# The gate of the experts' rows: both factors multiplied onto the MLP's result in PSUM, in place of one product in SBUF

## The chip, the cores and the metric

The kernel runs on one core of one Trainium2 chip, all in float32. A core has TensorE (PE; PEld is its weight load), VectorE (DVE), ScalarE (ACT), GpSimd (POOL) and a queue that issues DMAs (SP). Each engine runs its own instructions in program order and waits on the others by semaphores. The metric is the device time of one execution in microseconds (us): 1550.95 us before the change, the median of three runs (1548.26 to 1552.72).

## The reference, cut to what matters

```python
xn = layernorm(x)                                  # 2 x 2048 tokens of 256
s = mamba_and_mlp(xn)                              # x1 = xn + mamba(rmsnorm(xn)); s = x1 + mlp(rmsnorm(x1))
g = silu(moe(xn))                                  # 8 experts, the top 2 of each token, weighted
return x + s * g
```

`silu(v)` is `v * sigmoid(v)`, which is `h * (tanh(h) + 1)` with `h = v / 2`. The kernel holds `h` (the experts' two rows of a token, with weights that are already halved, added) in the tile `yk[0]` and `tanh(h)` in the tile `yk[1]`. The gate `g` thus has two factors, `yk[0]` and `yk[1] + 1`, and the last lines of the kernel compute `out = x + s * g`.

## The kernel before, in words

**Stages.** 4096 tokens are cut into 8 blocks (`c`) of 512. After an opening (norms, routing, the scatter of rows to experts) one long loop runs the Mamba recurrence: for each block, each of 4 groups of 128 channels (`d`) and each of 8 pairs of states (`g`), 256 steps in all. In each step DVE makes `b` (L1361, a product of `du` in PSUM and `B` in SBUF) and runs two scans into `h` (L1365); POOL multiplies `h` by `C` (L1295) and adds the pair (L1297); PE sums over the states into `y` in PSUM (L1267); ACT makes the exponentials `da` (L1254) and saves last columns (`hs`, L1291). At the start of each group DVE makes `du` from two SBUF tiles (L1358).

**Work drawn in beside it.** A generator hands out PE work of the feed-forward parts between the steps: first 39 tiles of 256 rows for the experts (`Expert`), then 16 tiles of 256 tokens for the MLP (`Mlp`, `c` and `hf`). The change touches only the last ones; in the trace their first multiplication starts at 1072.3 us, after the last of the experts. I number them 1 to 16.

**One MLP tile.** `pair` makes the hidden layer (PE `phm` L854, ACT tanh L1026, DVE product into `hidm` L1028); `second` multiplies with the second weights into `pom` (PE L866), in the PSUM bank "o", of which there is one, shared with the output projection of the Mamba part (`po`, L762). `gather` (L1044 on) has POOL issue four indirect DMAs of the experts' rows into `yk` (L1058), and puts later work on a list: `weigh` (ACT L1072, POOL addition L1076), `tanh` (ACT L1080) and `gate` (DVE L1083), due 5, 7 and 8 half-steps after the gather. There is a single pair of `yk` tiles: the next gather is issued only after `end` has cleared `yk_taken`, and its DMAs wait until the tile that they write was read for the last time.

**The end of one tile.** `finish` puts `total` (DVE L1094: `pom` times 0.5 plus `x1`), and that puts `end`: DVE L1101 (`pom` times `yk[0]`, which holds the whole gate by then), DVE L1102 (plus `x`, into an SBUF tile) and the store (SP L1105). If the gate has not been issued by then, `end` draws work from the list until it has.

**What sets the order.** `later` (class `Later`) is a list sorted by due time; `tick` and each half-step of the loop run what is due. The place of an instruction in its engine's queue is thus fixed when the program is built. In 11 of the 16 tiles the gate (L1083) stands directly ahead of L1101 in DVE's queue: `end` drew it there, or it was due there; in the tiles 3, 4, 6, 9 and 10 it stands earlier, with other DVE work between the two.

Of the kernel before, what the change touches and what calls it, by code (L numbers as in the profile page):

```python
# [11 lines left out]
ALU = mybir.AluOpType  # L12
# [37 lines left out]
def kernel(  # L50
# [18 lines left out]
    nc = tc.nc  # L69
# [107 lines left out]
    def act_table(name):  # L177

        if table[0] != name:
            nc.scalar.preload_act_table_set(name)  # L180
            table[0] = name
# [171 lines left out]
    later = Later()  # L353
# [12 lines left out]
    def drop(tag, n):  # L366
        gone.setdefault(tag, set()).add(n)
# [5 lines left out]
    def ring(tag, bufs):  # L373

        n = take(tag)
        later.free(tag, n - bufs)
        return tag, n
# [537 lines left out]
    class Expert(Ffn):  # L915
# [44 lines left out]
        def finish(self, po, n):  # L960
            i = self.i
            no = ring("ys", 2)
            expert_rows.append(no)
            ys = rows.tile([P, JS, DM], F32, tag="ys", name=f"ys{i}")
            later.put(
                lambda: nc.vector.tensor_tensor(  # L966
                    ys, po, self.b2.unsqueeze(1).to_broadcast([P, JS, DM]), ALU.add
                ),
                n, after=2,
            )  # L970
            later.put(
                lambda: nc.sync.dma_start(
                    ys_d[ts(i, TS), :].rearrange("(j p) d -> p j d", p=P), ys
                ),
                no, after=4,
            )
# [4 lines left out]
    class Mlp(Ffn):  # L981
# [61 lines left out]
        def gather(self):  # L1043

            c, hf = self.c, self.hf
            i0 = c * J + hf * JS
            yk_taken.append(self.name)
            if not yk_tiles:
                for k in range(TOPK):
                    yk_tiles.append(  # L1050
                        wpool.tile([P, JS, DM], F32, tag=f"w{k + 1}", name=f"yk{k}", bufs=5)
                    )
            yk = self.yk = yk_tiles
            for no in expert_rows:
                later.free(*no)
            for j in range(JS):
                for k in range(TOPK):
                    nc.gpsimd.indirect_dma_start(  # L1058
                        out=yk[k][:, j, :], out_offset=None, in_=ys_d,
                        in_offset=bass.IndirectOffsetOnAxis(  # L1060
                            ap=row_y[:, k, i0 + j : i0 + j + 1], axis=0
                        ),
                    )
            self.nxo = ring("ys", 2)
            self.xo = rows.tile([P, JS, DM], F32, tag="ys", name=f"xo{self.name}")
            self.tok = slice(c * T + hf * TS, c * T + (hf + 1) * TS)
            nc.sync.dma_start(self.xo, x[self.tok, :].rearrange("(j p) d -> p j d", p=P))

            def weigh():
                for j in range(JS):  # L1070
                    for k in range(TOPK):
                        nc.scalar.activation(  # L1072
                            yk[k][:, j, :], yk[k][:, j, :], AF.Copy,
                            scale=prob[:, k, i0 + j : i0 + j + 1],
                        )
                nc.gpsimd.tensor_tensor(yk[0], yk[0], yk[1], ALU.add)  # L1076

            def tanh():
                act_table(WITH_TANH)
                nc.scalar.activation(yk[1], yk[0], AF.Tanh)  # L1080

            def gate():
                nc.vector.scalar_tensor_tensor(yk[0], yk[1], 1.0, yk[0], ALU.add, ALU.mult)  # L1083
                self.gated = True

            later.put(weigh, after=5)
            later.put(tanh, after=7)
            later.put(gate, after=8)

        def finish(self, po, n):  # L1090
            x1, yk, xo = self.x1, self.yk, self.xo

            def total():
                nc.vector.scalar_tensor_tensor(po, po, 0.5, x1, ALU.mult, ALU.add)  # L1094
                drop("x1", self.n_x1)
                later.put(end, n)

            def end():
                while not self.gated:
                    later.next()  # L1100
                nc.vector.tensor_tensor(po, po, yk[0], ALU.mult)  # L1101
                nc.vector.tensor_tensor(xo, po, xo, ALU.add)  # L1102
                yk_taken.clear()
                later.put(
                    lambda: nc.sync.dma_start(  # L1105
                        out[self.tok, :].rearrange("(j p) d -> p j d", p=P), xo
                    ),
                    self.nxo, after=3,
                )

            later.put(total)
# [338 lines left out]
```

## Time and profile before

| | |
|---|---|
| median of three runs | 1550.95 us (1548.26 to 1552.72) |
| the profiled execution | 1551.53 us, its span 1549.8 us |
| mean granted TensorE clock | 0.948 |
| busy: PE, DVE, POOL, ACT | 1396.0, 1244.3, 1154.8, 919.8 us |
| DVE L1083, the gate, 16 times | 20.2 us, mean 1261 ns, from 665 to 2175 |
| idle of DVE just before L1083 | 13.8 us in 6 of them, on ACT's tanh |
| DVE L1101 and L1102, 16 times each | 11.1 us each |
| stage of the MLP tiles | from 1072.3 us; the last scan ends at 1486.3 us |

The span runs from the first to the last instruction of the profiled execution. "Idle before" is time in which the engine stood still ahead of an instruction, with what ended the wait. "Busy" contains whatever an instruction spends blocked once it has started, so that one and the same operation can show different durations.

### The profile page before, as it was taken

The numbers are of one execution on the slowest core, as the hardware profiler recorded it, in microseconds if no ns is written. First come the engines' busy times: TensorE is split into PE (matmuls) and PEld (weight loads), VectorE is DVE, ScalarE is ACT, GpSimd is POOL, SyncE is SP. The second block draws the span as 40 slices with busy tenths as digits, with TensorE's granted clock in tenths as the row PEclk, the third lists the DMA queues.
The fourth block names the chain that finished last, engine by engine and source line by source line (L and its number), as shares of the span: only waits on it lengthen the run. The fifth ranks groups of instructions, "written<-read, shape, count | busy, mean of one in ns | idle before, by whom it ended". The sixth has DMA issues, their size and how long they took to land. (4 is left out here: it accounts for less than half of the span.)

```text
span 1549.8 us, 18158 instructions
## 1 busy us (share of the span) xinstructions
PE 1396.0 (90%) x5246; PEld 982.9 (63%) x5246; DVE 1244.3 (80%) x1362; ACT 919.8 (59%) x1890; POOL 1154.8 (75%) x775
## 2 busy tenths in 40 slices
PE   6747999998999999999999999999888988899667
PEld 4524677666676577667766777667555656667436
DVE  7558887797788977799879777986898788899942
ACT  4846676575656764477557655676465664475322
POOL 2777689768786689679977897688865778677741
PEclk9558999999999999999999999999998999999888
DMA  5594347723592438524853467345610125412100
GB/s 188 206 378 162 94 141 250 268 86 110 165 343 86 129 115 288 199 87 144 271 214 118 129 217 283 92 125 186 225 48 27 49 68 208 131 35 68 55 14 28
DMA packets 171108, 233.70 MB, mean 151 GB/s; under 512 B 19824, under 2 KB 141552, under 8 KB 171008
## 3 DMA queue, kind: packets, MB, share of 16 engines
q1 hardware_dynamic: 164864, 215.75, 42.0%
q0 software_dynamic: 6144, 16.79, 3.2%
q8 instruction: 42, 0.69, 0.2%
q14 instruction: 58, 0.48, 0.1%
HBM read 196.04 MB, written 36.44 MB: 150 GB/s over the span
## 5 line engine op out<-in xcount | busy, mean ns | idle before, releaser
L1295 POOL TENSOR_TENSOR h<-h,C 128x1024 f32<-128x1024 f32 x256 | 608.7, 2379 | 230.9 <-ACT hs L1291 187.4
L1365 DVE TENSOR_TENSOR_SCAN h<-da,hs,b 128x512 f32<-128x512 f32 x384 | 479.0, 1271 | 42.7 <-PE y L1267 17.6
L1254 ACT ACTIVATE da<-dt,a_neg 128x512 f32<-128x512 f32 x512 | 358.2, 718 | 41.6 <-DVE h L1365 41.2
L1267 PE MATMUL y<-h,ident 128*128 128x512 f32 x594 | 304.9, 616 | 32.4 <-POOL h L1295 18.3
L1361 DVE TENSOR_TENSOR b<-du,B 128x1024 f32<-128x1024 f32 x256 | 314.7, 1229 | 19.3 <-DMA B<-bcd 13.3
L854 PE MATMUL phe<-xsTe,w_e 128*128 128x256 f32 x1248 | 290.8, 385 | 13.5 <-ACT hide L954 8.9
L854 PEld LDWEIGHTS phe<-xsTe,w_e 128*128 128x128 f32 x1248 | 239.1, 192 | 81.5 <-issue 25.6
L866 PE MATMUL poe<-w_e,hide 128*128 128x256 f32 x1248 | 289.2, 380 | 0.0
L1297 POOL TENSOR_TENSOR h<-h 128x512 f32<-128x512 f32 x215 | 276.4, 1286 | 16.9
L866 PEld LDWEIGHTS poe<-w_e,hide 128*128 128x128 f32 x1248 | 236.0, 191 | 65.1 <-issue 33.6
L954 ACT ACTIVATE hide<-phe,b 128x256 f32<-128x256 f32 x312 | 129.3, 469 | 129.3 <-PE phe L854 129.1
L1267 PEld LDWEIGHTS y<-h,ident 128*128 128x128 f32 x594 | 112.9, 197 | 122.9 <-issue 66.0
L1365 DVE TENSOR_TENSOR_SCAN h<-da,b 128x512 f32<-128x512 f32 x128 | 151.2, 1210 | 11.2 <-PE y L1267 3.2
L854 PE MATMUL phm<-xsTm,w_m 128*128 128x256 f32 x512 | 125.2, 397 | 21.4 <-DVE hidm L1028 20.8
L854 PEld LDWEIGHTS phm<-xsTm,w_m 128*128 128x128 f32 x512 | 100.6, 198 | 48.9 <-DVE hidm L1028 25.9
L866 PE MATMUL pom<-w_m,hidm 128*128 128x256 f32 x512 | 122.0, 390 | 3.1 <-DVE xom L1102 3.0
L866 PEld LDWEIGHTS pom<-w_m,hidm 128*128 128x128 f32 x512 | 100.0, 197 | 31.8 <-issue 14.4
L1291 ACT COPY hs<-h 128x2 f32<-128x2 f32 x192 | 36.1, 188 | 99.6 <-DVE h L1365 99.4
L459 POOL DMA_INDIRECT xs_d<-xt,slot x64 | 63.3, 989 | 38.7 <-DVE scratch L441 19.8
L1058 POOL DMA_INDIRECT yk<-ys_d,row_y x64 | 61.6, 962 | 38.6 <-DVE pom L1101 21.3
L582 DVE SCALAR_TENSOR_TENSOR xc<-px,par_sb,xc 128x512 f32<-128x512 f32 x96 | 71.5, 746 | 16.6 <-ACT xc L574 11.7
L966 DVE TENSOR_TENSOR ys<-poe,b 128x512 f32<-128x512 f32 x39 | 26.6, 682 | 58.8 <-PE poe L866 51.9
(175 smaller groups left out, 1438.3 us busy)
## 6 DMA issues: line engine op xcount, KB each, us to landing
w_e<-in_w SPq DMA_DIRECT2D x312, 256.0 KB, 3.5
B<-bcd SPq DMA_DIRECT2D x64, 512.0 KB, 6.9
C<-bcd SPq DMA_DIRECT2D x64, 512.0 KB, 7.3
xs<-xs_d SPq DMA_DIRECT2D x39, 256.0 KB, 2.7
ys_d<-ys SPq DMA_DIRECT2D x39, 256.0 KB, 4.2
b<-in_b SPq DMA_DIRECT2D x39, 128.0 KB, 4.1
xnr<-xnd SPq DMA_DIRECT2D x16, 256.0 KB, 7.5
xom<-in_x SPq DMA_DIRECT2D x16, 256.0 KB, 3.3
```

The lines of the kernel that those rows point to most:

```text
L459: r = nc.gpsimd.indirect_dma_start(out=xs_d, out_offset=bass.IndirectOffsetOnAxis(ap=slot[:, k, i : i + 1], axis=0), in_=x_of(i // J, i % ...
L582: nc.vector.scalar_tensor_tensor(v[:, s : s + T], px, conv_w[:, d, KC - 1 - s : KC - s], v[:, s : s + T], ALU.mult, ALU.add,)
L854: nc.tensor.matmul(ph[:, q, :], self.w1[c0 // 2][:, k, ts(q, P)], self.xT[:, k, :], start=(k == 0), stop=(k == KM - 1),)
L866: nc.tensor.matmul(po[:, j, :], self.hid[c // 2][:, c % 2, ts(j, P)], self.w2[c // 2][:, c % 2, :], start=(c == 0 and j == 0), stop=(c == ...
L954: nc.scalar.activation(hc[:, q, :], ph[:, q, :], AF.Relu, bias=self.b1[:, c0 + q : c0 + q + 1])
L1058: nc.gpsimd.indirect_dma_start(out=yk[k][:, j, :], out_offset=None, in_=ys_d, in_offset=bass.IndirectOffsetOnAxis(ap=row_y[:, k, i0 + j : ...
L1254: nc.scalar.activation(das[n][:, q, :], dts[c, d], AF.Exp, scale=a_neg[:, d, 2 * g + q : 2 * g + q + 1])
L1267: nc.tensor.matmul(ys[c, d], ident, hts[n][:, q, :], start=False, stop=(g == DS // 2 - 1 and q == nq - 1),)
L1295: nc.gpsimd.tensor_tensor(hts[n], hts[n], bct[c, "C", g], ALU.mult)
L1297: nc.gpsimd.tensor_tensor(hts[n][:, 0, :], hts[n][:, 0, :], hts[n][:, 1, :], ALU.add)
L1361: nc.vector.tensor_tensor(inp, dus[c, d].unsqueeze(1).to_broadcast([P, 2, T]), bct[c, "B", g], ALU.mult,)
L1365: nc.vector.tensor_tensor_scan(hts[n][:, q, :], das[n][:, q, :], inp[:, q, :], 0.0 if c % CPB == 0 else hs[c - 1][:, d, 2 * g + q : 2 * g ...
```

## The change

The product in SBUF is taken away, and its first factor goes onto `pom` in PSUM in `end`, as a third operation there. The tile counts as gated when the tanh is issued.

```diff
             def tanh():
                 act_table(WITH_TANH)
                 nc.scalar.activation(yk[1], yk[0], AF.Tanh)
-
-            def gate():
-                nc.vector.scalar_tensor_tensor(yk[0], yk[1], 1.0, yk[0], ALU.add, ALU.mult)
                 self.gated = True
 
             later.put(weigh, after=5)
             later.put(tanh, after=7)
-            later.put(gate, after=8)
...
             def end():
                 while not self.gated:
                     later.next()
+
+                nc.vector.scalar_tensor_tensor(po, yk[1], 1.0, po, ALU.add, ALU.mult)
                 nc.vector.tensor_tensor(po, po, yk[0], ALU.mult)
                 nc.vector.tensor_tensor(xo, po, xo, ALU.add)
```

The number of DVE instructions stays the same: 16 `scalar_tensor_tensor` from SBUF, SBUF to SBUF go, 16 from SBUF, PSUM to PSUM come. The queues of PE, ACT, POOL and SP keep all their instructions in the same order. DVE's queue differs only in the place of these 16: in 11 tiles the new one stands exactly where the old one stood, and in the tiles 3, 4, 6, 9 and 10 it moves later, to just ahead of L1101. The new operation waits for the tanh and for L1094; `yk[1]` is now read last by it, and `yk[0]` by L1101 as before.

## The prediction, blind

> **What bounds the kernel now.** I read the page first, then the source view of the gate's line, then the timeline around each of its 16 executions, and last what PE waited for. Times in parentheses are starts in the trace. No engine bounds alone: PE is busy for 90% of the span, DVE 80%, POOL 75%, and the chain that ended last passes from one to the other. The gate's line is on it:
>
> ```profile
> PE 18%; DVE 10%; POOL 8%; issue 4%; ACT 3%; DMA 1%; SPq 0%; DVEq 0%; POOLq 0%; ACTq 0%
> DVE h L1365 4%; PE y L1267 4%; POOL h L1295 3%; PE poe L866 3%; PE pom L866 3%; PE phe L854 2%; DVE b L1361 2%; PE phm L854 2%; PE po L762 2%; POOL yk L1058 2%; POOL h L1297 1%; DVE xc L582 1%; DVE yk L1083 1%; POOL ls L648 1%; POOL dt L649 1%
> ```
>
> One per cent of 1550 us is 16 us, and all of L1083 is 20.2 us busy. The next view is that of its line (least, middle and longest time in ns, then the idle time ahead of it):
>
> ```profile
> L1083 DVE SCALAR_TENSOR_TENSOR yk<-yk,yk x16: 665/892/2175, 1098.6 to 1544.6; 128x512 f32<-128x512 f32 x16
> ...
>   ACT yk L1080: 13.8, 6
> ```
>
> The same operation on tiles of one size takes 665 or 2175 ns. The timeline of tile 1 shows why (start, us, engine, line):
>
> ```profile
> 1097.85 2.36 POOL L1295 TENSOR_TENSOR h<-h,C 128x1024 f32<-128x1024 f32 x1
> ...
> 1098.59 2.16 DVE L1083 SCALAR_TENSOR_TENSOR yk<-yk,yk 128x512 f32<-128x512 f32 x1 [1.12 <-ACT yk L1080]
> ...
> 1100.79 0.70 DVE L1101 TENSOR_TENSOR pom<-pom,yk 128x512 f32<-128x512 f32 x1
> ```
>
> POOL's product ends at 1100.21; the gate ends at 1100.75, some 0.55 us later. It has stood blocked behind POOL and then run. The four other long ones on the path that I walked end in the same way after an L1295. So a DVE operation with two SBUF inputs waits for a running POOL product. The nearest rows of the form that the change brings do not show this:
>
> ```profile
> L1028 DVE SCALAR_TENSOR_TENSOR hidm<-hidm,phm x64: 660/664/689, 1074.7 to 1533.7; 128x512 f32<-128x512 f32 x64
> ```
>
> L1028 has one input in SBUF and one in PSUM, runs 64 times beside POOL's products, and never exceeds 689 ns. L1094, which writes to PSUM as the new operation does, takes 673 to 700 ns.
>
> **Who waits for a late DVE.** PE, at the second half of the next tile's hidden layer, as these rows show (the last bracket is PE's idle time and its releaser):
>
> ```profile
> 1105.30 2.91 PE L854 MATMUL phm<-xsTm,w_m 128*128 128x256 f32 x8 [2.85 <-DVE hidm L1028]
> ...
> 1244.75 2.42 PE L854 MATMUL phm<-xsTm,w_m 128*128 128x256 f32 x8 [3.29 <-DVE hidm L1028]
> 1271.58 1.99 PE L854 MATMUL phm<-xsTm,w_m 128*128 128x256 f32 x8 [3.36 <-DVE hidm L1028]
> 1296.57 3.03 PE L854 MATMUL phm<-xsTm,w_m 128*128 128x256 f32 x8 [4.47 <-DVE hidm L1028]
> ...
> 1381.50 1.99 PE L854 MATMUL phm<-xsTm,w_m 128*128 128x256 f32 x8 [0.28 <-DVE hidm L1028]
> 1442.18 1.99 PE L854 MATMUL phm<-xsTm,w_m 128*128 128x256 f32 x8 [1.19 <-DVE hidm L1028]
> ```
>
> They follow the `end` of tiles 1, 5, 6, 7, 10 and 13. There DVE is on the path, and PE moves by what DVE gains or loses, up to the wait shown.
>
> **The change, part by part.** *The operation itself.* The new one steps to its successor in 0.73 us, as L1094 and L1101 do when the next reads their result. The old one took, from its start to that of L1101: 2.20 (tile 1), 2.21 (5), 2.20 (7), 1.65 (13), 1.13 (8), and 0.70 to 0.73 in the other tiles where both are neighbours. Its place in the queue is the same there, so I take the differences: 1.47 + 1.48 + 1.47 + 0.92 = 5.3 us for tiles 1, 5, 7 and 13. Tile 8's 0.40 I cost at nothing: PE runs without a wait from 1296.6 to 1319.7 and covers it; without that cover it would be 0.4 more gain. The gate's price on an idle POOL (0.67) and the new one's (0.70) are equal for this purpose.
>
> [...]
>
> *Waits.* The new operation waits for the tanh as the old one did. In tiles 1, 5, 7 and 15 that wait (1.12, 1.02, 3.09 and 0.85 us) stays where it is, with L1101, L1102 and the scans queued behind. In tiles 4 and 6 (2.98 and 4.72 us) it goes, since the operation moves past it. In tile 4 nothing comes of it: DVE next waits 4.49 us for PE's `pom` (1211.12), and PE there waits for ACT (`pxd`, 1197.03). In tile 6, L1094 (1265.27) can start once PE ends `pom` at 1262.0, but `du` (L1358, two SBUF inputs) is then blocked by POOL's L1295 until 1264.8; walking on, `hidm` comes 0.9 us earlier if nothing else shifts. Bounds 0 and 0.9; I take 0.5.
>
> *Moved instructions.* In tiles 3, 9 and 10 the new one stands late, where its 0.73 us lies in front of work that PE waits for, and the 0.58 freed earlier is repaid only in tiles 3 and 9, inside unbroken DVE work. That costs 0.15 twice. In tile 10 L1094 (1375.22) starts when PE has finished, whatever DVE saved before, so 0.73 is lost in full. Sum of losses 1.0. POOL's next gather waits for L1101; it comes 0.7 later in tiles 3 and 10, which adds to POOL's idle 3.50 and 0.84 us, but about 1.4 earlier after tiles 5 and 7. No queue but DVE's changes order; the store on SP just follows L1102.
>
> *The `du` behind tile 1.* This is the largest single term and the least certain:
>
> ```profile
> 1106.93 5.09 DVE L1358 TENSOR_TENSOR du<-dt,xc 128x512 f32<-128x512 f32 x1
> ```
>
> ```profile
> 1105.84 0.94 POOL L1058 DMA_INDIRECT yk<-ys_d,row_y  x1 [0.30 <-issue]
> 1106.79 4.67 POOL L1295 TENSOR_TENSOR h<-h,C 128x1024 f32<-128x1024 f32 x2
> ```
>
> It starts 0.14 us after POOL has begun two products without a gap, and stands blocked for both. With DVE 1.47 us earlier it starts at 1105.46, while POOL still issues its gather; another `du` (1317.61) ran beside such an issue in 0.69 us. POOL's pair starts no earlier than about 1106.4, since the gather follows the L1297 before it, which gains 0.33 us. So `du` would be done before the pair, and DVE would gain 4.4 us more. PE can use only part: after 1125.0 it waits 2.80 us for L1102 (bank "o", L762) and 1.41 us for `sz` (L1275), in all 4.2 us, of which 1.47 is counted. I take 2.7; bounds 0 and 4.4.
>
> [...]
>
> *Sum.* 5.3 + 0.5 - 1.0 + 2.7 = 7.5 us. Nothing ahead of 1098 us and nothing in the tail changes: the gates of tiles 15 and 16 (1531.65, 1544.56) take 0.69 and 0.68 us with POOL at rest. From the profiled execution, 1551.5 - 7.5 = **1544.0 us**. Its 1551.53 lies 0.6 above the median of the three runs, well inside their spread of 4.5.
>
> **Rivals.** *`du` stays blocked* (chance 0.22): POOL comes earlier too, or DVE later. Against it stands the margin of about 1 us. The time is 1551.5 - 4.8 = 1546.7 us.
>
> *The gain is absorbed* (0.20): another engine is late next. For: from 1345 to 1420 PE is busy 74.2 of 75.0 us, and at tile 4 the path runs through ACT and PE without DVE. Against: PE's queue keeps its order, so an earlier start of PE there is an earlier end. If about 1.5 us is left, 1550.0 us.
>
> *It does not do what it says* (0.05): the new operation is blocked as well, say by its one SBUF input. Then only the moves count, with their 1.0 us of loss: 1552.5 us. Against: 64 executions of L1028.
>
> *Slower: other `du`s meet a pair of products* (0.13). Everything after 1100 us shifts against POOL by up to 1.5 us. A `du` that arrives behind a fresh pair costs 5.09 - 0.67 = 4.4 us, at the start of a group, where scans and PE hang on it. Seven more `du`s come after 1110 us; the trace shows them between 0.68 and 2.74, and POOL pairs at 1131.96, 1180.29, 1249.67 and 1281.91 that none of them meets. With the first still blocked, two more give 1546.7 + 8.8 = 1555.5, three 1560 us; from the third on the kernel is clearly slower.
>
> **How the numbers follow.** The forecast has 0.40, the rivals 0.22, 0.20, 0.05 and 0.13. A difference of 0.3% (4.65 us from the median, so 1546.3 and 1555.6) is about what a measurement of this kernel can tell from no change. Faster by more: most of the forecast (0.38) and near half of the first rival (0.10), with a little of the third case, 0.50. Slower by more: 0.12. Within: 0.38. The range goes down to 1540.5 (2.7 becomes 4.4, 0.5 becomes 0.9, and another blocked `du`, such as the 2.74 at 1155.62, comes free for part of it) and up to 1553.0, which takes in the absorbed and the blocked case and leaves out the slower one. The forecast's own range is 1541 to 1546.
>
> **What would show it.** Right: the new operation at 0.70 us in all 16, never near 2 us; `du` behind tile 1 below 1 us; PE's wait for `hidm` behind tiles 5, 7 and 13 shorter by 1.5, 1.5 and 0.9 us; DVE's busy time lower by some 9 us from this line alone (20.2 - 11.2). Wrong: the same durations but an end of the last scan (now 1486.3) that has hardly moved; then look for a later `du`, or for PE's waits on L1102. New long `du`s would show the slower rival.

## The result, and the profile after

Changed kernel: **1543.63 us** median of ten runs (1538.80 to 1546.68); the kernel before beside it: 1552.21 us (ten runs, 1548.26 to 1553.52). The ratio is 0.9942, its 95% interval 0.9927 to 0.9958, so 6.5 to 11.3 us less. The ten times of the changed kernel fall into two groups, four from 1538.8 to 1539.7 us at a mean granted clock of 0.954 and six from 1543.3 to 1546.7 us at 0.945 to 0.950. The profiled execution took 1545.81 us, its span is 1544.1 us. Lines from the change on stand lower by 2 (4 for L1094): L1098 is the new operation, L1099 and L1100 are the old L1101 and L1102, L1090 is `total`, L1293 POOL's product, L1356 `du`.

The source view of the new operation (times in ns: least, middle, most):

```profile
L1098 DVE SCALAR_TENSOR_TENSOR pom<-yk,pom x16: 672/674/697, 1102.7 to 1538.7; 128x512 f32<-128x512 f32 x16
```

Where the old one went from 665 to 2175 ns, all 16 now take 0.67 to 0.70 us. The timeline of tile 1 shows the same place in the queue, beside the same product of POOL:

```profile
1101.91 2.36 POOL L1293 TENSOR_TENSOR h<-h,C 128x1024 f32<-128x1024 f32 x1
1102.65 0.70 DVE L1098 SCALAR_TENSOR_TENSOR pom<-yk,pom 128x512 f32<-128x512 f32 x1 [1.06 <-ACT yk L1080]
```

The operation begins 0.74 us into the product, as the old one did, and is done 0.92 us before the product ends. What became of the `du` behind it is seen a little later:

```profile
1109.58 0.95 POOL L1058 DMA_INDIRECT yk<-ys_d,row_y  x1 [0.30 <-issue]
1109.60 0.71 DVE L1356 TENSOR_TENSOR du<-dt,xc 128x512 f32<-128x512 f32 x1
...
1110.54 2.36 POOL L1293 TENSOR_TENSOR h<-h,C 128x1024 f32<-128x1024 f32 x1
```

It runs during the last issue of the gather and ends at 1110.31, 0.23 us before POOL's next product: 0.71 us in place of 5.09. PE's waits for `hidm` behind the tiles 1, 5, 6, 7, 10 and 13, in the timeline of PE (the bracket is the idle time ahead):

```profile
1107.97 1.99 PE L854 MATMUL phm<-xsTm,w_m 128*128 128x256 f32 x8 [1.39 <-DVE hidm L1028]
...
1240.77 1.99 PE L854 MATMUL phm<-xsTm,w_m 128*128 128x256 f32 x8 [0.36 <-DVE hidm L1028]
1265.14 1.99 PE L854 MATMUL phm<-xsTm,w_m 128*128 128x256 f32 x8 [2.59 <-DVE hidm L1028]
1289.05 3.78 PE L854 MATMUL phm<-xsTm,w_m 128*128 128x256 f32 x8 [3.38 <-DVE hidm L1028]
...
1376.44 1.99 PE L854 MATMUL phm<-xsTm,w_m 128*128 128x256 f32 x8 [1.18 <-DVE hidm L1028]
1436.34 1.99 PE L854 MATMUL phm<-xsTm,w_m 128*128 128x256 f32 x8 [0.33 <-DVE hidm L1028]
```

They are shorter by 1.46, 2.93, 0.77, 1.09 and 0.86 us, and longer by 0.90 behind tile 10, where the operation has moved late. One row does not fit: behind tile 7 the same eight multiplications take 3.78 us, and 1.99 in the other five. That comes back below. Over all tiles the page has 14.1 us of idle time of L854 on `hidm`, against 20.8 before. DVE's busy time fell from 1244.3 to 1233.2 us.

**A measure for the experiments.** The time of a run holds stretches that the change does not touch and that vary on their own. From the first `du` to the 24th (the last before tile 1) the profile of before has 976.7 us, that of the changed kernel 979.9, with the same instructions, and the experiments below have 976.6 to 982.8. So each experiment is given by two numbers: the ratio of its time to that of the kernel before on the same chip, and the **stage**, from the start of the 24th `du` to the end of the last scan in its profile: 431.14 us before, 420.54 after.

### The profile page after: what moved, and what is told of

Same layout as the page of the kernel before. It is cut to its first block, busy times and chain, and to the rows that moved or that the text cites. A ratio compares the mean times of both kernels' runs of the same rounds, so it can differ in the third digit from the quotient of the medians.

```text
span 1544.1 us, 18175 instructions
## 1 busy us (share of the span) xinstructions
PE 1394.2 (90%) x5246; PEld 982.3 (64%) x5246; DVE 1233.2 (80%) x1362; ACT 919.6 (60%) x1890; POOL 1152.6 (75%) x775
## 5 line engine op out<-in xcount | busy, mean ns | idle before, releaser
L1293 POOL TENSOR_TENSOR h<-h,C 128x1024 f32<-128x1024 f32 x256 | 607.8, 2376 | 223.3 <-ACT hs L1289 183.5
L1359 DVE TENSOR_TENSOR b<-du,B 128x1024 f32<-128x1024 f32 x256 | 314.8, 1230 | 19.8 <-DMA B<-bcd 13.7
L854 PE MATMUL phe<-xsTe,w_e 128*128 128x256 f32 x1248 | 289.7, 384 | 12.4 <-ACT hide L954 8.8
L854 PEld LDWEIGHTS phe<-xsTe,w_e 128*128 128x128 f32 x1248 | 238.1, 192 | 80.3 <-issue 26.1
L1363 DVE TENSOR_TENSOR_SCAN h<-da,b 128x512 f32<-128x512 f32 x128 | 151.2, 1210 | 11.2 <-PE y L1265 3.2
L854 PE MATMUL phm<-xsTm,w_m 128*128 128x256 f32 x512 | 123.2, 393 | 14.8 <-DVE hidm L1028 14.1
L854 PEld LDWEIGHTS phm<-xsTm,w_m 128*128 128x128 f32 x512 | 99.9, 197 | 41.8 <-DVE hidm L1028 19.6
L582 DVE SCALAR_TENSOR_TENSOR xc<-px,par_sb,xc 128x512 f32<-128x512 f32 x96 | 71.5, 747 | 18.4 <-ACT xc L574 12.9
```

The costliest lines, as they stand in the source:

```text
L582: nc.vector.scalar_tensor_tensor(v[:, s : s + T], px, conv_w[:, d, KC - 1 - s : KC - s], v[:, s : s + T], ALU.mult, ALU.add,)
L854: nc.tensor.matmul(ph[:, q, :], self.w1[c0 // 2][:, k, ts(q, P)], self.xT[:, k, :], start=(k == 0), stop=(k == KM - 1),)
L1293: nc.gpsimd.tensor_tensor(hts[n], hts[n], bct[c, "C", g], ALU.mult)
L1359: nc.vector.tensor_tensor(inp, dus[c, d].unsqueeze(1).to_broadcast([P, 2, T]), bct[c, "B", g], ALU.mult,)
L1363: nc.vector.tensor_tensor_scan(hts[n][:, q, :], das[n][:, q, :], inp[:, q, :], 0.0 if c % CPB == 0 else hs[c - 1][:, d, 2 * g + q : 2 * g ...
```

## The experiments

**Theory A (the prediction's).** A DVE operation with two SBUF inputs waits for a running product of POOL; the gain comes from one input having gone to PSUM, at the gate itself and at the `du` that it delayed. **Rival B.** It comes from the place: the operation stands later in DVE's queue in five tiles, and the tanh no longer holds up what stood between. **C**, within A: how much of it is `du` alone.

**1. The late place, but in SBUF.** The order of every queue is that of the changed kernel.

```diff
-                nc.vector.scalar_tensor_tensor(po, yk[1], 1.0, po, ALU.add, ALU.mult)
+                nc.vector.scalar_tensor_tensor(yk[0], yk[1], 1.0, yk[0], ALU.add, ALU.mult)
```

> The gate is issued where the changed kernel has its new operation, directly ahead of the product with the MLP's result, but it multiplies in SBUF as before (yk[0] = (yk[1] + 1) * yk[0]). DVE's order is that of the changed kernel, only the operands differ. Theory A (the gain comes from an operation that POOL cannot block): the gate shows durations up to about 2.2 us again, mean above 1.1 us; in place of the 9.0 us that the changed kernel gained, 0 to 3 us are left, from the waits for the tanh that are gone in tiles 4 and 6. Theory B (the gain comes from the later place): as the changed kernel, 7 to 10 us faster than before.

Measured: 1567.72 us against 1563.7, ratio 1.0018 (1.0002 to 1.0033); stage 427.93, 3.2 us below before. In time the kernel is thus 0.3 to 5.2 us slower, where 0 to 3 us of gain were expected. The timeline has both blocked operations back, at tile 1 and at the `du` behind it:

```profile
1120.82 2.35 POOL L1293 TENSOR_TENSOR h<-h,C 128x1024 f32<-128x1024 f32 x1
1121.55 2.17 DVE L1098 SCALAR_TENSOR_TENSOR yk<-yk,yk 128x512 f32<-128x512 f32 x1 [1.23 <-ACT yk L1080]
...
1129.78 4.67 POOL L1293 TENSOR_TENSOR h<-h,C 128x1024 f32<-128x1024 f32 x2
1129.90 5.11 DVE L1356 TENSOR_TENSOR du<-dt,xc 128x512 f32<-128x512 f32 x1
```

The place alone brings no time that shows; B falls as the main cause.

**2. The old place, with one input in PSUM.** The other half of the same pair. The second factor `yk[0]` is replaced by the `du` tile in PSUM, so the gate's values are not the reference's.

```diff
-                nc.vector.scalar_tensor_tensor(yk[0], yk[1], 1.0, yk[0], ALU.add, ALU.mult)
+                du = list(dus.values())[-1]
+                nc.vector.scalar_tensor_tensor(yk[0], yk[1], 1.0, du, ALU.add, ALU.mult)
```

> The gate stands where the kernel before has it, but its second input is the tile du in PSUM in place of yk[0] (the factor yk[0] of the gate is thus left out and du's values stand in its place; the count, sizes and order of all operations stay). Theory A: its 16 executions take about 0.67 us each, none over 0.75; the kernel gains 5 to 9 us, the du of block 6 behind tile 1 takes below 1 us. The waits of 3.0 and 4.7 us for the tanh in tiles 4 and 6 stay. Theory B: no gain, within 2 us of the kernel before.

Measured: 1557.71 us, ratio 0.9953 (0.9935 to 0.9972); stage 417.12. Its source view:

```profile
L1084 DVE SCALAR_TENSOR_TENSOR yk<-yk,du x16: 661/664/690, 1119.3 to 1550.6; 128x512 f32<-128x512 f32 x16
```

No queue has changed, only one operand; all 16 run unblocked, and the gain is there. A holds.

**3. Tile 1 alone.** The new form for tile 1, the old one for the other 15.

```diff
+            self.in_psum = 2 * c + hf == 0
...
+                if self.in_psum:
+                    nc.vector.scalar_tensor_tensor(po, yk[1], 1.0, po, ALU.add, ALU.mult)
```

> Only the first of the 16 MLP tiles is changed; the other 15 keep the gate in SBUF. Theory A with the du behind it as its largest term: the du of block 6 takes 0.7 us in place of 5.1, and 4 to 6 us of the 9.0 are there with this one instruction. If the terms are as they were predicted, 1.5 + 2.7 = 4.2 us. If the du in the trace of before was chance of that one execution: about 1.5 us. Theory B: nothing, since in this tile the place does not change.

Measured: 1556.84 us, ratio 0.9950 (0.9934 to 0.9967); stage 423.94, 7.2 below before. One operation of 16 accounts for most of what the time shows.

**4. The `du` behind tile 1 alone.** The gate stays; that one `du` gets an input in PSUM, and takes 0.69 us in place of 5.09. Its values are those of another group's tile, and one group's results differ from the reference.

```diff
-                    dus[c, d] = ps_1.tile([P, T], F32, tag="du", name=f"du{c}_{d}")
-                    nc.vector.tensor_tensor(dus[c, d], dts[c, d], xcs[c, d], ALU.mult)
+                    other = xcs[c, d]
+                    if (c, d) == (6, 0):
+                        dus[c, d] = other = dus[5, ND - 1]
+                    else:
+                        dus[c, d] = ps_1.tile([P, T], F32, tag="du", name=f"du{c}_{d}")
+                    nc.vector.tensor_tensor(dus[c, d], dts[c, d], other, ALU.mult)
```

> The kernel before with one instruction changed: the du of block 6, group 0 takes the old du in PSUM in place of xc as its second input (one group's values are thus others), so that POOL cannot block it. All gates stay in SBUF. Theory A: this du takes 0.7 us, and the kernel gains 2.7 to 4.4 us, which is the share of the change that is not the gate's own. If that blocked du is chance of the one profiled execution, or if PE is late anyway: below 1.5 us. Theory B: nothing.

Measured: 1561.15 us, ratio 0.9979 (0.9962 to 0.9996), 0.6 to 5.9 us; stage 424.66. PE's waits behind tile 1 and at the next output projection, in the timeline of PE:

```profile
1121.25 3.01 PE L854 MATMUL phm<-xsTm,w_m 128*128 128x256 f32 x8 [2.92 <-DVE hidm L1028]
...
1143.62 2.42 PE L762 MATMUL po<-ow_sb,sz 128*128 128x256 f32 x10 [1.41 <-DVE sz L1275]
```

The wait of 2.80 us for L1102 at that projection is gone, the 1.41 us for `sz` stays as it was. The wait in the first row is as long as in the kernel before (2.92 and 2.85 us), since tile 1's gate is still blocked.

**5 to 8. The rest of the parts, and other forms**, as a second group, with the changed kernel again (5) as their measure. Kernel 6 keeps the old product in the five tiles whose operation moves (3, 4, 6, 9, 10); kernel 7 keeps it in tile 1; kernel 8 keeps the old place in all 16, but lets ACT write the tanh into a PSUM bank. The code is cut; in 6 and 7 the rest is as in 3.

```diff
# 6
+            self.in_psum = 2 * c + hf + 1 not in (3, 4, 6, 9, 10)
# 7
+            self.in_psum = 2 * c + hf != 0
# 8
+                th, n = bank("h", [P, JS, DM], f"th{self.name}")
...
-                nc.scalar.activation(yk[1], yk[0], AF.Tanh)
+                nc.scalar.activation(th, yk[0], AF.Tanh)
...
-                nc.vector.scalar_tensor_tensor(yk[0], yk[1], 1.0, yk[0], ALU.add, ALU.mult)
+                nc.vector.scalar_tensor_tensor(yk[0], th, 1.0, yk[0], ALU.add, ALU.mult)
+                drop(*n)
```

> The changed kernel once more, on the same chip as the three beside it. Its opening (to the du of the sixth block's last group) runs the same instructions as before but differed by 4.1 us between the two first profiles and by 15 to 23 us on another chip, so the stage is read from that du's start to the end of the last scan: 431.1 us before, 420.5 after. Theory A: the stage is again 10 to 11 us shorter than before, whatever the opening does; the total gains 7 to 11 us. If the 10.6 was chance of one execution: another figure by over 2 us.

> Only the 11 tiles are changed in which the new operation stands in the old one's place; the tiles 3, 4, 6, 9 and 10 keep the gate in SBUF at its early place. As predicted (operations 5.3, du 2.7, moves 0.5 - 1.0 = -0.5): 8.0 us less in the stage, 0.5 more gain than the full change. If the moved tiles bring something by themselves (their blocked gates of 1.7 to 2.1 us and the waits of 3.0 and 4.7 us gone, as 3.2 us of the late place in SBUF suggest): the stage is 2 to 4 us longer than the changed kernel's 420.5.

> All tiles but the first are changed. Theory A: the du behind tile 1 stays blocked for 5.1 us, and the stage keeps what does not hang on it: 10.6 less the 7.2 that tile 1 alone gave, so 3 to 5 us shorter than before, 426 to 428 us. If the terms were independent of tile 1's du and of equal size: 15/16 of the gain, 421 us.

> A version that keeps the product early and takes only the lock away: ACT writes the tanh into a bank of the PSUM ring h, and the gate multiplies it onto yk[0] in SBUF at the place of the kernel before; no operation is added to the end of a tile. Theory A, from the early gate with an operand in PSUM (stage 417.1 us): gates at 0.67 us each, the stage 12 to 15 us shorter than before, 416 to 419 us, and 2 to 4 us below the changed kernel; the total 9 to 13 us below before. Rival: the ring of three banks is short while it holds the tanh, PE waits for a bank in each of 16 tiles for about a microsecond, and the gain falls to 0 to 6 us.

| kernel | us (before 1551.96) | ratio, interval | stage, us |
|---|---|---|---|
| 5 changed, again | 1541.24 | 0.9927 (0.9910 to 0.9944) | 420.59 |
| 6 five moved tiles as before | 1544.01 | 0.9947 (0.9927 to 0.9966) | 417.68 |
| 7 all but tile 1 | 1546.95 | 0.9968 (0.9951 to 0.9985) | 422.49 |
| 8 tanh in PSUM, old place | 1543.38 | 0.9942 (0.9926 to 0.9958) | 418.32 |

Kernel 7 shows that tile 1 is worth about half. Kernel 6 is a riddle: its stage is 2.9 us *shorter* than that of the changed kernel, as if the moves cost that much, while its time is longer by 2.8 us. Kernel 8 is as good as the change within the intervals, which again speaks for A: with one input outside SBUF the gates take 0.66 to 0.69 us, whether the other values come from `du` (2) or from ACT (8).

**9 to 12. Do the moves cost 2.9 us?** The moves alone; the two forms mixed (the five tiles with kernel 8's tanh in PSUM at the old place, the rest as in the change); and kernel 6 and the changed kernel again.

```diff
# 9
+            self.in_psum = 2 * c + hf + 1 in (3, 4, 6, 9, 10)
# 10
+            self.in_psum = 2 * c + hf + 1 not in (3, 4, 6, 9, 10)
...
+                th = yk[1]
+                if not self.in_psum:
+                    th, n = bank("h", [P, JS, DM], f"th{self.name}")
```

> The moves alone: in tiles 3, 4, 6, 9 and 10 the factor goes late and onto PSUM, in the other 11 the old product in SBUF stays where it stood. If the lock is all that counts, the blocked gates of tiles 1, 5, 7 and 13 stay and the moved ones bring at most their own blocked time (1.06 + 1.14 + 1.39 us in tiles 4, 6 and 10), of which the path sees little: the stage from the 24th du to the last scan stays within 2 us of the kernel before (431.1), or up to 3 us longer if the late place itself costs the 2.9 us by which the changed kernel lags behind the version that keeps the five tiles as they were. If place is worth nothing and the lag came from where the half-clock intervals of TensorE fall, the stage is no longer than before.

> Tiles 3, 4, 6, 9 and 10 keep the early gate, but with its tanh in PSUM, so that it has one SBUF input; the other 11 tiles as in the changed kernel. If lock and place both count, the stage is at most that of the version that keeps the five tiles blocked (417.7 us), by up to 3 us shorter; all 16 new operations take 0.66 to 0.70 us. In time: 0.1 to 0.4% below the changed kernel. If the lag of the changed kernel is an accident of the TensorE clock, it can land anywhere from 416 to 421 us.

> The version that changes only the 11 tiles, once more, on the chip of the changed kernel: a stage of 417.7 us again if the difference belongs to the program; 420 or more if it was the run. In time 0.19% (2.9 us) below the changed kernel, if the stage decides.

> The changed kernel, on the same chip, as the measure for the other three: stage 420.5 us, time 0.6% below the kernel before.

| kernel | us (before 1565.08) | ratio, interval | stage, us |
|---|---|---|---|
| 9 moves alone | 1565.91 | 1.0000 (0.9986 to 1.0013) | 426.17 |
| 10 mixed | 1556.08 | 0.9944 (0.9931 to 0.9957) | 419.12 |
| 11 kernel 6 again | 1556.27 | 0.9948 (0.9935 to 0.9961) | 417.47 |
| 12 changed, a third time | 1552.80 | 0.9932 (0.9917 to 0.9948) | 415.55 |

The last row overturns the reading of kernel 6: the changed kernel itself has 420.5, 420.6 and 415.6 us. So a stage of one profile is not good to 3 us, and the loss against kernel 6 is no evidence of a cost of the moves. No version beats the change; kernels 6, 8 and 10 can't be told from it.

**Where the 5 us between two profiles of one program lie.** Up to tile 5 the third profile is 1.3 us ahead, which arises between tile 2 and the 27th `du`, in a row of PE that is shown further below. Between the tiles 7 and 8 the profile after loses 0.8 us on before, and the third gains 2.0. PE's row there stood out above. The windows view of the profile after (us, busy time of PE with its count, granted clock, DMA share, GB/s):

```profile
1284.90:1288.30 3.40, 0.77 (x2) 0.94 0.59 214
1288.30:1291.70 3.40, 2.65 (x6) 0.50 0.80 214
```

In the first window PE was busy for 0.77 of 3.40 us; in the second its clock is halved (the stretch lasts 6.8 us), and the eight multiplications take 3.78 us. In the third profile the same multiplications come after a wait of 1.68 us and run at the full clock, first their row, then the windows:

```profile
1300.13 1.99 PE L854 MATMUL phm<-xsTm,w_m 128*128 128x256 f32 x8 [1.68 <-DVE hidm L1028]
```

```profile
1298.10:1301.50 3.40, 1.72 (x7) 1.00 0.93 245
1301.50:1304.90 3.40, 3.40 (x14) 1.00 0.88 307
```

The kernel before has such stretches as well, here behind tiles 5 and 7:

```profile
1243.10:1246.50 3.40, 1.75 (x7) 0.95 0.71 224
1246.50:1249.90 3.40, 3.40 (x6) 0.54 0.14 39
1294.30:1297.70 3.40, 1.13 (x5) 0.95 0.87 281
1297.70:1301.10 3.40, 3.40 (x10) 0.54 0.79 277
```

Kernel 4 changes nothing near either of them, and yet gains 1.69 and 1.68 us there: half of 3.4 us, since it has no half-clock stretch at either place.

## Why the prediction was right, and where its terms were off

The table follows the stage: the start of L1102 (L1100) of some tiles, of two `du` and the end of the last scan, each from the 24th `du` on, minus the same in before (us). The third profile of the change stands for it as well, since it has fewer half-clock stretches. All columns are set against the one profile that there is of the kernel before, with the stretches that it happens to have.

| point | du alone (4) | moves alone (9) | all but 1 (7) | tile 1 alone (3) | no moves (6) | after | third (12) |
|---|---|---|---|---|---|---|---|
| tile 1 | +0.10 | +0.04 | 0.00 | -1.43 | -1.40 | -1.40 | -1.41 |
| tile 2 | -2.96 | +0.05 | +0.09 | -5.80 | -5.70 | -5.71 | -5.72 |
| tile 3 | -2.96 | -0.83 | -0.63 | -5.80 | -5.70 | -6.59 | -6.59 |
| 27th du | -3.19 | -2.09 | -1.49 | -6.21 | -5.75 | -6.63 | -7.88 |
| tile 5 | -3.17 | -2.10 | -2.94 | -6.25 | -7.18 | -8.05 | -9.33 |
| 28th du | -4.86 | -6.83 | -7.67 | -7.94 | -8.87 | -12.79 | -14.06 |
| tile 7 | -4.84 | -4.24 | -6.50 | -7.96 | -10.30 | -11.59 | -12.88 |
| tile 8 | -6.52 | -5.92 | -8.54 | -9.65 | -12.33 | -10.83 | -14.91 |
| tile 11 | -6.47 | -5.00 | -7.45 | -7.17 | -12.27 | -9.05 | -14.05 |
| tile 13 | -6.47 | -4.97 | -8.32 | -7.19 | -13.13 | -9.92 | -14.91 |
| last scan | -6.48 | -4.97 | -8.65 | -7.20 | -13.46 | -10.60 | -15.59 |

**The operation itself, 5.3 us: right.** Tile 1 gives 1.40, tile 5 1.42 (after, from the 27th `du` on), tile 7 1.41 (from tile 5 to 7: kernel 6 3.12, kernel 3 1.71), tile 13 0.87 (after, from tile 11 on). Together 5.1; the 0.2 less come from the new operation's step to its successor, 0.78 to 0.80 us in these tiles in place of the 0.73 reckoned.

**Tile 8's 0.40 at nothing: wrong by 0.35.** Between the tiles 7 and 8, the kernels 6, 7 and 12, which change tile 8, gain 2.03 or 2.04 us; the kernels 3, 4 and 9, which do not, gain 1.68 or 1.69. The PE rows of 4, 6, 9 and 12 run at full clock between these tiles (L854 behind tile 7 in 1.99 to 2.00 us), and 3 and 7 gain the same. PE's cover there did not hold it back.

**Tile 6, 0.5: right.** From tile 5 to 7 the moves alone gain 2.14, kernel 3 gains 1.71: 0.43. The `du` after it does get blocked, as the walk had it (2.54 us in place of 1.16), and still some is left.

**Moved instructions, 1.0 lost: right for the tiles 9 and 10, wrong for tile 3.** From tile 8 to 11 the third profile loses 0.86 us and the moves alone 0.92, where 0.88 was reckoned for tiles 9 and 10. But at tile 3, where 0.15 was to be lost, the moves *gain*. With the gate of tile 3 no longer ahead of it, the 26th `du` starts before POOL's product rather than behind its start; first the kernel before, then the changed one:

```profile
1155.45 2.36 POOL L1295 TENSOR_TENSOR h<-h,C 128x1024 f32<-128x1024 f32 x1 [2.33 <-ACT hs L1291]
1155.62 2.74 DVE L1358 TENSOR_TENSOR du<-dt,xc 128x512 f32<-128x512 f32 x1
```

```profile
1153.45 0.69 DVE L1356 TENSOR_TENSOR du<-dt,xc 128x512 f32<-128x512 f32 x1
1153.81 2.54 POOL L1293 TENSOR_TENSOR h<-h,C 128x1024 f32<-128x1024 f32 x1 [2.47 <-ACT hs L1289]
```

That frees 2.05 us of DVE, on top of the 0.58 of the gate that has moved. At its next L582 DVE then waits 0.77 us for ACT's `xc`, which leaves it 1.65 us ahead; about 0.8 of that is lost again up to L1100, most of it to the new operation, and 0.87 arrives at tile 3. All profiles of the changed kernel and of the moves alone show it (0.86 to 0.88 from tile 2 to 3), kernel 6 shows 0.00. Up to the 27th `du` it is 0.92 in the first profile and 0.89 in the second, but 2.16 in the third and 2.14 in the moves alone. That difference is no work of the moves. It is `pxd` (L602) in between, at half clock in the kernel before and in the first profile (5.33 us in both), at full clock in the third and in kernel 9 (3.63 us); here before and the third:

```profile
1197.03 5.33 PE L602 MATMUL pxd<-xc,xp_sb 128*48 128x512 f32 x8 [2.08 <-ACT xc L596]
```

```profile
1207.28 3.63 PE L602 MATMUL pxd<-xc,xp_sb 128*48 128x512 f32 x8 [2.09 <-ACT xc L596]
```

So 0.9 us of gain belongs to the moves there. The prediction walked the moves of tiles 3 and 4 past PE's waits, and named the 26th `du` only as something that the range might hold. A 32nd `du` (1.43 to 0.68) adds 0.68 at the end in the same way, with tile 13.

**The `du` behind tile 1, 2.7 us: the term that was mis-sized.** It came free for the reason given, and DVE got 4.38 us. At tile 2 4.31 of it have arrived (5.71 - 1.40), nearly the upper bound of 4.4. The step that failed is "PE can use only part". It set the gain against two waits of PE, 2.80 and 1.41 us, and took the multiplications between the waits as fixed. They are not: in the kernel before, PE runs at half clock behind its wait of 2.85 us for `hidm`. Two more rows and the clock before (first the 3.41 us up to the start of the stretch), then the same two rows after:

```profile
1108.00 1.84 PE L1267 MATMUL y<-h,ident 128*128 128x512 f32 x2
1127.79 1.53 PE L762 MATMUL po<-ow_sb,sz 128*128 128x256 f32 x6 [2.80 <-DVE xom L1102]
```

```profile
1102.82:1106.23 3.41, 0.93 (x4) 1.00 0.72 199
1106.23:1109.64 3.41, 3.41 (x7) 0.50 0.99 326
```

```profile
1109.80 1.02 PE L1265 MATMUL y<-h,ident 128*128 128x512 f32 x2
1126.15 1.53 PE L762 MATMUL po<-ow_sb,sz 128*128 128x256 f32 x6 [0.24 <-DVE xom L1100]
```

With a wait of 1.39 us no half-clock stretch follows. L854 then takes 1.99 us in place of 2.91 and the next row 1.02 in place of 1.84, together 1.74 less. The waits fall by 1.46 (`hidm`) and 2.56 (L1102), and the three make 5.76 us, against 5.71 at tile 2. The wait for `sz` stays at 1.41, since `sz` is itself DVE's, behind L1102 in its queue, and moves with it. So the waits alone gave 2.56, close to the 2.7, but by two slips that cancel: 1.41 for `sz` was counted in, and 1.47 was taken off that had come out of another wait. What was put at nothing is the 1.74 us of clock.

Two kernels with tile 1 still blocked bear this out. In kernel 4 the wait stays (2.92 us) and the rows behind it are slow (3.01 and 1.74 us); of the same 4.4 us only 3.06 arrive at tile 2 (2.96 + 0.10), since DVE now waits for PE:

```profile
1136.61 0.70 DVE L1094 SCALAR_TENSOR_TENSOR pom<-pom,x1m 128x512 f32<-128x512 f32 x1 [1.25 <-PE pom L866]
```

In kernel 7 the gate of tile 1 (2.17 us) and `du` (5.10 us) are blocked as before, and nothing is gained at tile 2 (+0.09). The stretch behind tile 1 costs time here only once DVE is early: in the kernel before, PE still waits 2.80 us for L1102 behind the slow rows; in kernel 4 that wait is gone, and DVE waits 1.25 us for PE. The rows of L854 behind tile 1 show it in the kernel before and in 4 and 9 (2.91, 3.01 and 2.93 us), and not in after, 3, 6 and 12 (1.99 us in each). The gain at tile 2 is 5.68 to 5.92 us in all nine profiles with tile 1 unblocked.

**The sum.** 5.1 + 0.35 + 0.43 + 4.31 - 0.86 + 0.9 + 0.68 = 10.9 us, against 7.5 predicted. The third profile's 15.59 is that plus what its clock spares it against the one profile of before: 1.24 at `pxd` and 2 x 1.69 behind the tiles 5 and 7, in all 15.5. The first profile keeps 10.6, because it has the stretch at `pxd`, one at tile 7 (2.8 us against the third up to tile 8), and loses 0.9 more between tiles 9 and 11. In time the three groups show 8.6, 10.7 and 12.3 us between medians. That the forecast of 1544.0 came within 0.4 us of the first median is therefore in part luck: 3.4 us of gain were missing from its sum, and the medians differ by as much from group to group. The mechanism and the sign were right for the reasons given, the size was low.

**The rivals.** The new operation was never blocked, `du` came free, and the gain was not absorbed. Of the slower case two pieces came true, the 28th `du` at 2.54 us and the 31st at 1.83 in place of 1.36. Its price of 4.4 us for each `du` that meets a pair was too high: the 31st meets one in both kernels (before, the pair at 1406.23, which the prediction's list leaves out), and comes in after the first product. Of what was to be seen, the durations and PE's waits behind the tiles 7 and 13 came within half a microsecond; behind tile 5 the wait fell by 2.93 in place of 1.5. The line itself costs 10.9 us (16 x 0.681) in place of 20.2, against 11.2 reckoned.

**What stays open.** The moves as a whole: 1.0000 (0.9986 to 1.0013) alone, and 0.20 and 0.16% between the changed kernel and kernel 6 in the two groups, with intervals that overlap. Less the half-clock stretches at `pxd` and behind the tiles 5 and 7 (1.27 + 2 x 1.69), their stage gains 0.3 us (4.97 - 4.65), too little for these times to show; that of experiment 1, reckoned alike, loses 1.4, with the sign of its ratio. With one profile of the kernel before, how often its stretches come in its other executions is not known. The 0.9 us between tiles 9 and 11 goes with a half-clock stretch of 6.8 us in the first profile, where the 16 multiplications of L762 take 5.99 us, against 5.08 in the third; it was not followed row by row, and neither was the wait behind tile 5.

## What to carry to other kernels

Look for operations of one form and one size with very different durations. Here they went from 665 to 2175 ns, the long ones ended just behind a product of POOL, and one operand in PSUM brought all 16 to 0.66 to 0.69 us without moving anything (kernel 2). What such an operation delays can be worth more than itself (4.31 us against 1.40 behind tile 1): follow the next one with two SBUF inputs, and check whether it then starts before or behind the other engine's next product. When the gain of an engine is limited by another that waits for it, count more than the waits: look whether the rows behind a wait are slower than the same rows elsewhere, since a shorter wait can take that away as well (here 2.91 us became 1.99 as the wait went from 2.85 to 1.39). And do not settle 3 us on one profile each when PE has waits as here, of 1.4 to 4.8 us, behind some of which its clock was halved and behind others not.

## What the runs showed of the hardware

**The granted clock follows a grid of time.** In the stage of the two profiles, before and after, every stretch of half clock lasts 3.4 us or a multiple (6.8, 13.7), and in each of them the starts lie whole multiples of 3.41 us apart. The windows shown behind the tiles 5 and 7 lie 0.3 to 0.4 us off that grid. In the 3.41 us up to the start of the stretch PE was busy for 0.93 us behind tile 1, 1.43 and 0.81 behind the tiles 5 and 7 (before), and 1.16 behind tile 7 (after); after 1.72 in the window shown of the third profile the clock stayed full. Over the stage of the two profiles, of the windows of the grid at full clock the busiest that half clock followed had 1.56 us of busy time, and the idlest that it did not follow had 1.53; in between, busy time alone does not tell the two apart. Where a wait falls on the grid counts as well: in the kernel before, PE's wait of 2.85 us for `hidm` behind tile 1 left 0.93 us in one window, and half clock followed, while its wait of 2.80 us for L1102 fell across two, left 1.69 and 1.53, and it did not. A stretch costs up to 1.7 us where PE is on the path (1.69 behind the tiles 5 and 7). That is why 1.3 us between two profiles of one program became 4 us at tile 8.

**A block can last through a pair of products, but need not.** `du` stood still for two products of POOL that follow each other without a gap in before and in experiment 1 (5.09 and 5.11 us over a pair of 4.67). There it had started 0.14 and 0.12 us into the first product. In the experiments 7 and 9 it took 5.10 us at the same place. The 31st `du` starts 1.54 us into such a pair in before and 1.07 in after, and comes in after the first product, as here in before:

```profile
1406.23 5.12 POOL L1295 TENSOR_TENSOR h<-h,C 128x1024 f32<-128x1024 f32 x2
...
1407.77 1.36 DVE L1358 TENSOR_TENSOR du<-dt,xc 128x512 f32<-128x512 f32 x1
```

It ends 0.56 us after the first product, and the pair takes 5.12 us in place of 4.67. In the profile after it takes 1.83 us, and in all 14 profiles 1.34 to 1.83. So the prediction's "stands blocked for both" holds for the `du` behind tile 1 and not for every pair; what decides between the two cases is open. Beside POOL's issue of an indirect DMA `du` ran in 0.71 us. Reading one operand from PSUM, or from a PSUM tile that ACT wrote, was enough in all 96 gates of the six profiles that have all 16 of them that way (after, 2, 5, 8, 10 and 12; 0.66 to 0.70 us).
